# Layer 0 of a convolution-attention hybrid: the sums over whole cells as 64x64 matrices for two heads, and four buffers for the reciprocals

## The chip, the cores and the metric

The kernel runs on one core of one Trainium2 chip. The metric is the device time of the whole program in microseconds (us), from one launch, as the median of several runs. The engines are named as in the profile: PE is TensorE (matmuls), PEld its weight loads, DVE is VectorE, ACT is ScalarE, POOL is GpSimd, SP is SyncE, which here only issues DMAs. L816 means line 816 of the kernel before.

## The reference

The program has two layers on an image of 256 channels and 64 x 64 pixels, all in f32. The change is in layer 0 alone. There, after a group norm, q, k and v are made by 256 x 256 projections, q and k go through a sigmoid, and v is divided by its norm. There are 8 heads of 32 channels. For each pixel and each of three window sizes (64, 32 and 16 pixels wide) the products k vᵀ of all pixels in a box around the pixel are summed, and the pixel's q is multiplied with that sum and divided by q times the sum of k:

```
q = sigmoid(q); k = sigmoid(k); v = v / max(norm(v), 1e-12)
Ik = integral(k); Ikv = integral(einsum('bfhw,bghw->bfghw', k, v))
for w in (1, 2, 4):
    wk, wkv = box(Ik, 64 // w), box(Ikv, 64 // w)
    attn = einsum('bdhw,bdfhw->bfhw', q, wkv)
    outs.append(attn / (einsum('bdhw,bdhw->bhw', q, wk)[:, None] + 1e-6))
o = concatenate(outs); x = x + Wout @ o + bout
```

Layer 1 (softmax attention over 4096 tokens, then an expert layer with two experts per token) follows and is not touched.

## The kernel before, in words

**Cells.** The image is cut into cells of 8 x 8 pixels. A token's place is a strip `ix` of 8 columns (NCH = 8 strips of 512 tokens), a band `b` of 16 rows (NB = 4 bands of 128 tokens), and a half `u` of that band (one cell of 64 tokens). A box of 64, 32 or 16 pixels reaches `r` = 4, 2 or 1 cells to each side (`REACH`). For a query in a given cell, a box holds some cells entirely, for all queries of the cell alike; at its rims it cuts through others. Cells held entirely enter through their sum of k vᵀ: a 32 x 32 matrix for each head, prepared in `ssum[r]` for r = 4 and 2. Cells that are cut enter through scores: kᵀq for the cell, times a 0/1 mask, times v.

**Stages.** Heads are worked on in two halves of four (`g` = 0, 1), so that four heads fill 128 partitions. For each half, `prepare` makes q, k, v, the cell sums and the denominators (`rec`); `attend` then works through the windows in the order r = 2, r = 4, r = 1. For r = 2 and r = 4 it has two stages: first passes by rows of cells (bands 1, 2, 0, 3), then strips of columns, `ix` from 0 to 7. The change is in the passes by rows of cells.

**One pass.** Two PSUM banks, `accs[0]` and `accs[1]`, accumulate the two halves of a band, four heads on 128 partitions, 8 strips along the free dimension. The pass begins with the sums: for each u and ix, q of that cell times the sum of its whole cells. For r = 2 (L816) this is one 128 x 128 matrix for all four heads, with zeros off the diagonal, taken from the tile `blocks`. For r = 4 (L829) it is four 32 x 32 matrices straight from `ssum`. Then come steps of scores (L797, into four of six PSUM banks), masks (`masked`, L651 and L659), and the products with v (L841). The mask of heads 0 and 2 is applied by VectorE from PSUM; that of head 1, and of head 3 in every other step, by GpSimd from a copy that ScalarE makes. At the end ScalarE and VectorE copy the two banks into `raw` (L855).

**Order.** It is written out by hand. The matmuls of `use` (the sums, with the first step, and L841) are issued two steps after the scores that they go with (`behind`, `tick`). Besides, there is a list of `chores`, of which one is done after each step (`step_done`), and all that are left at the end of a pass (`finish`). `next_blocks` makes the chores that fill `blocks` for the next pass, one ScalarE activation for each head (L716): it copies the sums of all 8 strips and both halves, scaled by a 0/1 column that keeps one head's partitions. They are put at the front of the list as soon as the sums of the current pass are issued. `blocks` has one buffer, so the first of them waits until PE has read it. Other chores are the four parts of the reciprocal of `rec` (VectorE, L749), `turn_over` (which sends `rec` to DRAM and begins to fetch it back), and for each finished strip its division (L759, GpSimd) and its projection (L767).

**Reciprocals.** A division multiplies by `by`, a row of reciprocals spread over 32 partitions per head. SP fetches each by DMA (L738). There are two buffers; the next row is fetched when one has been used.

Of the kernel before, what the change touches and what calls it, by code (L numbers as in the profile page):

```python
# [22 lines left out]
F32 = mybir.dt.float32  # L23
# [7 lines left out]
P = 128  # L31
# [4 lines left out]
CH = 512  # L36
NCH = N // CH
# [4 lines left out]
CELL = SW * SW  # L42
D = 32
# [18 lines left out]
_MCELLS = [2 * r + 2 for r in REACH]  # L62
_MCELL0 = [sum(_MCELLS[:i]) for i in range(NW)]
_PARTS = {
    "": {"ident": P, "head": 4},
    "c": {"group": P, "xmask": 3 * SW, "ymask": SW * sum(_MCELLS), "ycut": 2 * SW},
    "k": {"sums": NCH // 4 * NW * D, "before8": CH, "sides": NB * (SW + IMG + 1)},
    "m": {"rank": NE, "iota": P, "before": P, "ones": P, "number": 1, "high": 2 * NT, "base": EARLY, "spare_early": 2 * EARLY, "spare": NU, "steps": N // SLOT, "unit": 3 * (NU - USUAL), "zero": 2 * NE},
# [1 line left out]
_AT, _W = {}, 0  # L70
# [6 lines left out]
def constants():  # L77

    out = np.zeros((P, _W), np.float32)
    p = np.arange(P)
    out[:, _AT["ident"]] = np.eye(P)
    out[:, _AT["group"]] = (p[:, None] // GRP == p[None, :] // GRP) / GRP
    out[:, _AT["head"]] = p[:, None] // D == np.arange(4)[None, :]
    a, b, c = p[:, None] % SW, p[:, None] // SW, np.arange(SW)[None, :]
    out[:, _AT["xmask"]] = np.concatenate([a >= 0 * c, a >= c, a < c], 1)
    rel = [np.arange(-SW * r, SW * r + BH)[None, :] for r in REACH]
    ys = [(b >= y - SW * r) & (b < y + SW * r) for r, y in zip(REACH, rel)]
    out[:, _AT["ymask"]] = np.concatenate(ys, 1)  # L90
    out[:, _AT["ycut"]] = np.concatenate([b % SW < c, b % SW >= c], 1)

    ns = range(NCH // 4 * NW)
    col = np.arange(D)[None, :]
    out[:, _AT["sums"]] = np.concatenate([col == 4 * n + p[:, None] // D for n in ns], 1)


    y, c = np.divmod(np.arange(CH)[None, :], SW)
    out[:, _AT["before8"]] = (b < y) & (a < c)
    c, y = np.arange(SW)[None, :], np.arange(IMG + 1)[None, :]  # L100
    out[:, _AT["sides"]] = np.concatenate(
        [np.concatenate([(a < c) & (b >= 0), BH * m + b < y], 1) for m in range(NB)], 1
    )
    out[:, _AT["rank"]] = NE - np.arange(NE)
    out[:, _AT["iota"]] = np.arange(P)
    out[:, _AT["before"]] = p[:, None] < p[None, :]
    out[:, _AT["ones"]] = 1
    out[:, _AT["number"]] = 1 + p[:, None]
    out[:, _AT["high"]] = np.arange(2 * NT)[None, :]
    out[:, _AT["base"]] = 1 + SLOT * np.arange(EARLY)  # L110
    spare = 1 + 2 * N + p[:, None] + P * np.arange(NU + 2 * EARLY)[None, :]
    out[:, _AT["spare"]], out[:, _AT["spare_early"]] = spare[:, :NU], spare[:, NU:]
    steps = SLOT * np.arange(N // SLOT)
    out[:, _AT["steps"]] = steps + np.minimum(steps, THIRD)
    unit = np.arange(USUAL, NU)
    out[:, _AT["unit"]] = np.concatenate([unit, (unit - THIRDS) // 2, unit - (unit - THIRDS) // 2])
    return out
# [3 lines left out]
def tile_conv_attn_hybrid(ctx: ExitStack, tc: tile.TileContext, a: dict, out: bass.AP):  # L121
    nc = tc.nc
# [15 lines left out]
    cst = constants_of("", const)  # L138
    ident = cst["ident"]
# [128 lines left out]
    with ExitStack() as phase:  # L268
# [28 lines left out]
        with (  # L297
# [3 lines left out]
            bank, _ = banks(ps)  # L301
# [323 lines left out]
        chores = []  # L625
# [70 lines left out]
        def attend(g, work, ps, qk, v, ssum, rec, woT):  # L696
# [3 lines left out]
            hs = [slice(D * h, D * (h + 1)) for h in range(4)]  # L700
            qcells = qT.rearrange("p (i n) -> p i n", n=CH)
# [1 line left out]

            blocks = work.tile([P, NCH, 2, 4, D], F32, name="blocks")
            passes = [(r, b) for r in (2,) for b in (1, 2, 0, 3)]

            def next_blocks():
                if not passes:  # L710
                    return []
                r, b = passes.pop(0)

                def block(h):
                    with tc.issue_after(latest_copy[0]) if latest_copy[0] else nullcontext():
                        nc.scalar.activation(  # L716
                            blocks[:, :, :, h, :],
                            ssum[r][:, :, 2 * b : 2 * b + 2, :],
                            AF.Copy,
                            scale=cst["head"][:, h : h + 1],  # L720
                        )

                return [lambda h=h: block(h) for h in range(4)]

            for f in next_blocks():
                f()
# [6 lines left out]
            def fetch():  # L733
                if order:
                    w, ix = order.pop(0)
                    by = work.tile([P, CH], F32, name="by", bufs=2)
                    row = D * (ix % 4) + 4 * (NCH // 4 * w + ix // 4)
                    nc.sync.dma_start(by, recs[row : row + 4, :].unsqueeze(1).to_broadcast([4, D, CH]))  # L738
                    held.append(by)

            def turn_over():
                nc.sync.dma_start(recs, rec)
                for _ in range(2):
                    fetch()

            def reciprocal(z):
# [7 lines left out]
            for w in windows:  # L754
                r = REACH[w]
# [22 lines left out]
                for b in (1, 2, 0, 3) if r > 1 else ():  # L778
                    accs = [bank() for _ in range(2)]
# [10 lines left out]
                    for step in steps:  # L790
                        scs = [score() for _ in range(4)]
                        at, places = 0, []
                        for n, i, lo, hi, kind in step:
                            for h in range(4):
                                for u in range(2):
                                    q0 = P * b + CELL * u
# [4 lines left out]
                                        start=True,  # L801
                                        stop=True,
                                        skip_group_check=True,
# [6 lines left out]
                        def use(places=places, sms=sms, accs=accs, begun=begun, b=b, last=step is steps[-1], raw=raw, r=r):  # L810
                            if not begun[0]:
                                begun[0] = True
                                if r == 2:
                                    for u, ix in ((u, ix) for u in range(2) for ix in range(NCH)):
                                        q0 = P * b + CELL * u
                                        nc.tensor.matmul(  # L816
                                            accs[u][:, CELL * ix : CELL * (ix + 1)],
                                            blocks[:, ix, u].rearrange("p h d -> p (h d)"),
                                            qcells[:, ix, q0 : q0 + CELL],
                                            start=ix == 0,  # L820
                                            stop=False,
                                            skip_group_check=True,
                                        )
                                    chores[:0] = next_blocks()
                                else:
                                    for u, ix in ((u, ix) for u in range(2) for ix in range(NCH)):
                                        for h in range(4):
                                            q0 = P * b + CELL * u
                                            nc.tensor.matmul(  # L829
                                                accs[u][hs[h], CELL * ix : CELL * (ix + 1)],  # L830
                                                ssum[r][hs[h], ix, 2 * b + u, :],
                                                qcells[hs[h], ix, q0 : q0 + CELL],
                                                start=ix == 0,
                                                stop=False,
                                                skip_group_check=True,
                                            )
                            for at, n, i, lo, hi, *_ in places:
                                for h in range(4):
                                    for u in range(2):
                                        us = slice(CELL * u, CELL * (u + 1))  # L840
                                        nc.tensor.matmul(  # L841
                                            accs[u][hs[h], CELL * lo : CELL * hi],
                                            v[us, i, hs[h]],
                                            sms[h][us, at : at + n],
                                            start=False,
                                            stop=last and at == places[-1][0],
                                            skip_group_check=True,
                                        )
                            if last:

                                finish()
                                for u in range(2):
                                    q0 = P * b + CELL * u

                                    (nc.vector.tensor_copy if u else nc.scalar.copy)(  # L855
                                        raw[:, :, q0 : q0 + CELL], accs[u].rearrange("p (i n) -> p i n", n=CELL)
                                    )
# [4 lines left out]
                for ix in range(NCH):  # L862
# [16 lines left out]
                    for step in steps:  # L879
                        scs = [score() for _ in range(4)]  # L880
                        at, places = 0, []
                        for n, i, c0, c1, *mk in step:

                            rows = CELL if len(step) == 1 else P
                            for h in range(4):
                                for u in range(0, P, rows):
# [4 lines left out]
                                        start=True,  # L891
                                        stop=True,
# [1262 lines left out]
```

## Time and profile before

| | |
|---|---|
| median of 3 runs | 2709.99 us (2706.1 to 2723.75) |
| profiled execution | 2709.02 us |
| its span, first to last instruction | 2707.1 us |
| PE busy | 2624.4 us (97%) |
| DVE busy | 1880.5 us (69%) |
| ACT busy | 1518.1 us (56%) |
| POOL busy | 817.9 us (30%) |
| mean granted TensorE clock | 0.990 |
| layer 0 in the span | up to about 964 us (last projection L767 at 964.4) |
| `attend`, first half: passes of r = 2, of r = 4 | about 128 to 189 us, about 260 to 324 us |
| `attend`, second half: the same | about 598 to 657 us, about 728 to 791 us |

How to read the profile's rows. A group of instructions has its line, engine, operation and tiles (output <- inputs), shapes (partitions x elements), a count, and the idle time of its engine before it, with what ended that idle time behind the arrow. For PE, 32\*64 means 32 rows and 64 columns of the array in use. An f32 matmul leaves two records, each a weight load and a matmul, so counts are twice those of the code. The busy time of overlapping matmuls is more than what passes by the clock; the time from one group's start to the next one's is the surer measure. In a table of stretches, each column is an engine's busy time with its number of instructions, and the granted clock is 1.00 at full speed.

### The profile page before, as it was taken

To read this page: it belongs to the slowest core of one execution; us is meant where nothing else is said; L and a number is where in the kernel's file an instruction comes from. 1 tells how busy PE (TensorE), PEld (TensorE's weight loads), DVE (VectorE), ACT (ScalarE), POOL (GpSimd) and SP (SyncE) were. 2 spreads that over 40 slices of the span, in tenths; PEclk is the share of its full clock that TensorE was granted. 3 is DMA by queue.
4 is the path that set the end of the run, shared out by engine and by line. 5 is a ranking of instruction groups with operands and counts; after the bars stand their busy time and mean duration, and the time that the engine had idled before them with its cause. 6 is when DMAs were issued, how large, how long until landed. Compare 5 with 4: busy or idle time off the path is not lost.

```text
span 2707.1 us, 70743 instructions
## 1 busy us (share of the span) xinstructions
PE 2624.4 (97%) x30398; PEld 1221.8 (45%) x30398; DVE 1880.5 (69%) x2570; ACT 1518.1 (56%) x2079; POOL 817.9 (30%) x919
## 2 busy tenths in 40 slices
PE   6999999999999999999999999999999999999995
PEld 5465436746544654111212121212121278888884
DVE  6868788586878866888888889888888871111114
ACT  3342323234232435999898989898989842222222
POOL 2067777306777731010000100000001122222220
PEclk9899999999999999999999999999999999999996
DMA  5000000000000000555555555555556645555555
GB/s 148 7 19 26 10 29 22 12 13 23 26 9 31 22 22 13 113 115 118 110 114 114 118 109 118 105 118 118 126 114 151 153 142 197 173 200 170 191 175 196
DMA packets 114461, 256.56 MB, mean 95 GB/s; under 512 B 19890, under 2 KB 76440, under 8 KB 100052
## 3 DMA queue, kind: packets, MB, share of 16 engines
q0 software_dynamic: 22240, 132.66, 23.4%
q1 hardware_dynamic: 84724, 110.30, 12.5%
q10 hardware_dynamic: 7168, 8.92, 1.0%
q8 instruction: 242, 3.96, 0.6%
q14 instruction: 87, 0.71, 0.1%
HBM read 118.64 MB, written 17.86 MB: 50 GB/s over the span
## 4 chain that ended last, share of the span: by engine, by line
PE 91%; DVE 4%; DMA 3%; issue 1%; ACT 1%; POOL 0%; ACTq 0%; SPq 0%; DVEq 0%; POOLq 0%
PE ps_three L1860 19%; PE ps_acc L1819 19%; PE ps_sc L887 8%; PE ps_yp L1528 8%; PE ps_hp L1511 7%; PE ps_acc L903 7%; PE ps_sc L767 3%; PE ps_sc L797 3%; PE ps_acc L841 3%; PE ps_two L441 2%; PE ps_mm L1303 2%; DMA yrows<-v,qk 2%; PE ps_two L534 1%; PE ps_acc L816 1%; PE ps_three L1794 1%; PE ps_mm L1318 1%
## 5 line engine op out<-in xcount | busy, mean ns | idle before, releaser
L1860 PE MATMUL ps_three<-qk 32*64 32x512 f32 x6144 | 563.2, 612 | 2.3 <-DVE t L1798 1.3
L1860 PE MATMUL ps_one<-qk 32*64 32x512 f32 x2048 | 556.3, 613 | 0.2 <-ACT pe L1869 0.2
L1892 DVE TENSOR_TENSOR act<-act,pe 128x2048 f32<-128x2048 f32 x195 | 447.3, 2294 | 82.5 <-ACT pe L1872 51.6
L1872 ACT ACTIVATE pe<-ps_three 128x1536 f32<-128x1536 f32 x330 | 477.3, 1446 | 0.0
L651 ACT COPY sm<-ps_sc 128x384 f32<-128x384 f32 (+2 forms) x418 | 212.9, 539 | 452.4 <-PE ps_sc L887 323.0
L659 DVE TENSOR_TENSOR sm<-ps_sc,mask 128x512 f32<-128x512 f32 (+3 forms) x788 | 343.3, 499 | 64.7 <-PE ps_sc L887 62.3
L659 POOL TENSOR_TENSOR sm<-sm,mask 128x192 f32<-128x192 f32 (+4 forms) x444 | 349.9, 819 | 113.3 <-ACT sm L651 113.2
L1892 DVE TENSOR_TENSOR act<-act 128x2048 f32<-128x2048 f32 x150 | 343.8, 2292 | 51.4 <-ACT act L1872 37.9
L1880 POOL DMA_DIRECT2D pe<-pe x108 | 93.4, 865 | 939.8 <-ACT pe L1872 610.4
L1819 PE MATMUL ps_acc<-pe,v 128*32 128x512 f32 x2640 | 351.6, 604 | 0.0
L1514 ACT ACTIVATE v<-ps_hp,qk 128x256 f32<-128x256 f32 (+1 forms) x256 | 123.1, 481 | 342.6 <-PE ps_hp L1511 342.6
L1860 PEld LDWEIGHTS ps_three<-qk 32*64 32x64 f32 x6144 | 112.6, 129 | 414.5 <-ACT pe L1869 244.0
L1872 ACT ACTIVATE act<-ps_three 128x1536 f32<-128x1536 f32 x182 | 263.1, 1446 | 0.0
L1528 PE MATMUL ps_yp<-qk,v 128*128 128x256 f32 (+1 forms) x1088 | 241.7, 380 | 0.0
L1511 PE MATMUL ps_hp<-qk 128*128 128x256 f32 (+1 forms) x1024 | 236.8, 389 | 2.8 <-ACT v L1514 1.7
L887 PE MATMUL ps_sc<-qk 32*128 32x256 f32 (+5 forms) x3456 | 233.2, 445 | 0.1
L1869 ACT ACTIVATE pe<-ps_one 128x512 f32<-128x512 f32 x330 | 197.5, 598 | 58.3 <-PE ps_one L1860 33.8
L1528 PEld LDWEIGHTS ps_yp<-qk,v 128*128 128x128 f32 (+1 forms) x1088 | 200.3, 187 | 30.7 <-issue 1.3
L903 PE MATMUL ps_acc<-sm,v 128*32 128x256 f32 (+4 forms) x2816 | 211.7, 407 | 0.1
L659 POOL TENSOR_TENSOR sm<-sm,ycut 128x512 f32<-128x512 f32 (+3 forms) x130 | 144.4, 1133 | 214.0 <-ACT sm L651 213.7
L1511 PEld LDWEIGHTS ps_hp<-qk 128*128 128x128 f32 x1024 | 180.7, 189 | 52.7 <-ACT v L1514 12.8
L1819 PE MATMUL ps_acc<-act,v 128*32 128x512 f32 x1456 | 193.9, 604 | 0.0
(364 smaller groups left out, 2908.8 us busy)
## 6 DMA issues: line engine op xcount, KB each, us to landing
pe<-pe POOLq DMA_DIRECT2D x108, 1024.0 KB, 7.6
qk<-in_L_ffn_W SPq DMA_DIRECT2D x64, 1024.0 KB
by<-recs SPq DMA_DIRECT2D x48, 256.0 KB
rows<-in_x SPq DMA_DIRECT2D x16, 256.0 KB
qk<-in_L_ffn_b SPq DMA_DIRECT2D x32, 128.0 KB
y<-yrows SPq DMA_DIRECT2D x8, 512.0 KB
y<-yrows ACTq DMA_DIRECT2D x8, 512.0 KB
rec<-recs SPq DMA_DIRECT2D x60, 64.0 KB
```

What stands on the lines that cost most here:

```text
L651: copied = nc.scalar.copy(sm[:, :used], sc[:, :used])
L659: done = engine.tensor_mul(to, of, mk.unsqueeze(1).to_broadcast(list(to.shape)))
L887: nc.tensor.matmul(scs[h][u : u + rows, at : at + n], kT[hs[h], P * i + u : P * i + u + rows], qT[hs[h], CH * ix + CELL * c0 : CH * ix + C ...
L903: nc.tensor.matmul(acc[hs[h], CELL * c0 : CELL * c1], v[:, i, hs[h]], sms[h][:, at : at + n], start=not begun[0], stop=last and at == plac ...
L1511: nc.tensor.matmul(hp[:, :n], w1[:, k, tok(m)], x_now[:, k, :n], start=k == 0, stop=k == KC - 1)
L1514: done["gelu"] = nc.scalar.activation(hid[:, m, :n], hp[:, :n], AF.Gelu, bias=cols[:, m : m + 1]).ins
L1528: product = nc.tensor.matmul(yp[:n], hid[:, m, P * j : P * j + n], w2[:, m, :], start=m == 0, stop=m == NH - 1)
L1819: nc.tensor.matmul(to[D * hd : D * (hd + 1), :], lhsT(hd), rhs(hd), start=start, stop=stop, skip_group_check=True,)
L1860: nc.tensor.matmul(to[CELL * u : CELL * (u + 1), :], qk[hs, 1, g, P * i + CELL * u : P * i + CELL * (u + 1)], qk[hs, 0, g, chunk(qc)], sta ...
L1869: first = nc.scalar.activation(head(pe, 0), one, AF.Exp, scale=C**-0.5)
L1872: nc.scalar.activation(pe[:, CH:], three.rearrange("p h n -> p (h n)"), AF.Exp, scale=C**-0.5).ins
L1892: latest[:] = [nc.vector.tensor_add(total, total, weights_of[r, i]).ins]
```

## The change

For both r = 2 and r = 4, the sums of a pass are now 64 x 64 matrices for two heads: two heads' 32 x 32 sums on the diagonal, zeros in the two other corners. Each pair (u, ix) has two of them, one for partitions 0 to 63 and one for partitions 64 to 127, each on its own rows and columns of the array. So a pass has 32 matmuls for its sums; it had 16 for r = 2 and 64 for r = 4.

`blocks` is half as large and is filled by two activations in place of four, one for the even and one for the odd heads, scaled by a new constant of two columns (`odd`). The list of passes it is filled for now includes r = 4: eight passes for each half of the heads. The fill for the first pass of r = 4 is added in the last pass of r = 2. The rows of reciprocals have four buffers instead of two, and four are fetched at first.

```diff
-    "": {"ident": P, "head": 4},
+    "": {"ident": P, "head": 4, "odd": 2},
...
+    out[:, _AT["odd"]] = p[:, None] // D % 2 == np.arange(2)[None, :]
...
-            blocks = work.tile([P, NCH, 2, 4, D], F32, name="blocks")
-            passes = [(r, b) for r in (2,) for b in (1, 2, 0, 3)]
+            blocks = work.tile([P, NCH, 2, 2, D], F32, name="blocks")
+            passes = [(r, b) for r in (2, 4) for b in (1, 2, 0, 3)]
...
-                            scale=cst["head"][:, h : h + 1],
+                            scale=cst["odd"][:, h : h + 1],
...
-                return [lambda h=h: block(h) for h in range(4)]
+                return [lambda h=h: block(h) for h in range(2)]
...
-                    by = work.tile([P, CH], F32, name="by", bufs=2)
+                    by = work.tile([P, CH], F32, name="by", bufs=4)
...
-                for _ in range(2):
+                for _ in range(4):
                     fetch()
...
-                                if r == 2:
-                                    for u, ix in ((u, ix) for u in range(2) for ix in range(NCH)):
-                                        q0 = P * b + CELL * u
+                                for u, ix in ((u, ix) for u in range(2) for ix in range(NCH)):
+                                    q0 = P * b + CELL * u
+                                    for two in (slice(0, 2 * D), slice(2 * D, 4 * D)):
                                         nc.tensor.matmul(
-                                            accs[u][:, CELL * ix : CELL * (ix + 1)],
-                                            blocks[:, ix, u].rearrange("p h d -> p (h d)"),
-                                            qcells[:, ix, q0 : q0 + CELL],
+                                            accs[u][two, CELL * ix : CELL * (ix + 1)],
+                                            blocks[two, ix, u].rearrange("p h d -> p (h d)"),
+                                            qcells[two, ix, q0 : q0 + CELL],
                                             start=ix == 0,
                                             stop=False,
                                             skip_group_check=True,
                                         )
-                                    chores[:0] = next_blocks()
-                                else:
-                                    for u, ix in ((u, ix) for u in range(2) for ix in range(NCH)):
-                                        for h in range(4):
-                                            q0 = P * b + CELL * u
-                                            nc.tensor.matmul(
-                                                accs[u][hs[h], CELL * ix : CELL * (ix + 1)],
-                                                ssum[r][hs[h], ix, 2 * b + u, :],
-                                                qcells[hs[h], ix, q0 : q0 + CELL],
...
+                                chores[:0] = next_blocks()
```

More of the change, by code (lines that the diff above doesn't have):

```diff
@@ L823, in use @@
                                         )
-                                    chores[:0] = next_blocks()
-                                else:
-                                    for u, ix in ((u, ix) for u in range(2) for ix in range(NCH)):
-                                        for h in range(4):
-                                            q0 = P * b + CELL * u
-                                            nc.tensor.matmul(
-                                                accs[u][hs[h], CELL * ix : CELL * (ix + 1)],
-                                                ssum[r][hs[h], ix, 2 * b + u, :],
-                                                qcells[hs[h], ix, q0 : q0 + CELL],
[L833 to L836, printed above, removed]
+                                chores[:0] = next_blocks()
                             for at, n, i, lo, hi, *_ in places:
```

## The prediction

> **What bounds the kernel now.** I read the chain that ended last first, since only time on it counts.
>
> ```profile
> PE 91%; DVE 4%; DMA 3%; issue 1%; ACT 1%; POOL 0%; ACTq 0%; SPq 0%; DVEq 0%; POOLq 0%
> PE ps_three L1860 19%; PE ps_acc L1819 19%; PE ps_sc L887 8%; PE ps_yp L1528 8%; PE ps_hp L1511 7%; PE ps_acc L903 7%; PE ps_sc L767 3%; PE ps_sc L797 3%; PE ps_acc L841 3%; PE ps_two L441 2%; PE ps_mm L1303 2%; DMA yrows<-v,qk 2%; PE ps_two L534 1%; PE ps_acc L816 1%; PE ps_three L1794 1%; PE ps_mm L1318 1%
> ```
>
> TensorE carries 91% of the chain. The line that the change removes, L816 (the sums of the passes with r = 2), is itself on it with 1%, about 27 us. Its counterpart for r = 4, L829, is not named. So the time rides on what these sums cost on PE. Next I cut the first half (g = 0) into stretches, each from one pass's sums to the next: four passes of r = 2, then two of r = 4.
>
> ```profile
> core 0: us, PE busy (x) PEld busy (x) DVE busy (x) ACT busy (x) POOL busy (x), PEclk, DMA share, GB/s
> 134.40:152.10 17.70, 16.81 (x549) 12.97 (x544) 11.22 (x21) 7.84 (x14) 11.21 (x12) 1.00 0.02 4
> 152.10:168.60 16.50, 16.18 (x537) 12.43 (x529) 9.41 (x19) 7.84 (x14) 10.40 (x12) 1.00 0.15 52
> 168.60:179.50 10.90, 9.59 (x297) 8.06 (x289) 6.56 (x13) 5.63 (x11) 5.84 (x6) 1.00 0.02 5
> 179.50:188.70 9.20, 9.20 (x208) 6.92 (x208) 3.19 (x9) 2.43 (x5) 3.86 (x6) 1.00 0.01 2
> 266.70:283.20 16.50, 15.93 (x432) 7.82 (x424) 11.40 (x20) 4.82 (x9) 10.60 (x10) 1.00 0.06 20
> 283.20:296.80 13.60, 13.60 (x424) 6.40 (x416) 9.21 (x17) 5.30 (x10) 10.62 (x10) 1.00 0.01 4
> ```
>
> PE is busy for nearly the whole of each stretch, at full granted clock (1.00); no other engine exceeds four fifths. Third, the timeline of PE around the sums of one pass of each kind: how long until the next kind of matmul starts, and what released it.
>
> ```profile
> 152.11 3.79 PE L816 MATMUL ps_acc<-qk,blocks 128*128 128x64 f32 x32
> 155.82 1.10 PE L841 MATMUL ps_acc<-sm,v 64*32 64x192 f32 x48
> ...
> 283.21 2.12 PE L829 MATMUL ps_acc<-qk,ssum 32*32 32x64 f32 x128
> 285.26 0.98 PE L841 MATMUL ps_acc<-sm,v 64*32 64x448 f32 x16
> ...
> 296.81 1.99 PE L829 MATMUL ps_acc<-qk,ssum 32*32 32x64 f32 x128
> 298.73 0.98 PE L841 MATMUL ps_acc<-sm,v 64*32 64x448 f32 x16
> ```
>
> From the first sum to the next L841, r = 2 takes 155.82 - 152.11 = 3.71 us (seven of its eight passes, the eighth 4.00 with a pause inside). r = 4 takes 298.73 - 296.81 = 1.92 us (six of eight; 2.05 and 2.67 where a pause fell in). In all, 30.0 and 16.2 us. Each f32 matmul has two records, so 16 matmuls make 32 and 64 make 128. The large form is the slow one. The reason shows in the instructions of single lines (durations are min/median/max):
>
> ```profile
> L816 PEld LDWEIGHTS ps_acc<-qk,blocks x256: 186/192/192, 134.4 to 650.5; 128*128 128x128 f32 x128
> L816 PE MATMUL ps_acc<-qk,blocks x256: 217/275/323, 134.4 to 650.6; 128*128 128x64 f32 x128
> ...
> L829 PEld LDWEIGHTS ps_acc<-qk,ssum x1024: 101/105/105, 266.7 to 779.7; 32*32 32x32 f32 x171
> L829 PE MATMUL ps_acc<-qk,ssum x1024: 211/214/238, 266.7 to 779.8; 32*32 32x64 f32 x171
> ...
> L797 PEld LDWEIGHTS ps_sc<-qk x2688: 127/131/227, 128.2 to 785.2; 32*64 32x64 f32 x192
> ```
>
> A load lasts 105, 131 and 192 ns for 32, 64 and 128 columns: some 77 ns of latency and 0.81 to 0.95 ns a column, so about 27, 54 and 110 ns of streaming. Matmuls of L829 and L816 stream 64 elements. Records of L829 start in fours, 56 ns from four to four, so 64 elements take about 56 ns. Pairs of L816 start 3.71/32 = 116 ns apart, which is its load: it is bound by weights, with the matmul hidden beside them.
>
> **The change part by part.** *The sums.* After it a pass of either kind has 16 places (8 column strips, 2 halves u), each with two 64x64 matmuls on separate rows and columns of the array: 32 matmuls, 64 pairs of records. Neither row shows a 64x64 form, so it is bounded from both sides. If both tiles run together and each load runs beside the matmul ahead of it, a round of two records costs the longer of 54 (load) and 56 (stream), and a pass has 32 rounds, as L829 has now (4 tiles a round). That gives L829's 1.92 us plus a longer first load (27 ns): 1.95 us. From above: nothing overlaps, 64 x (54 + 56) = 7.0 us.
>
> Two rules of the Trainium skill speak against the low end. *TensorE: Matmul & The Clock Gate* (Part 3, "What overlaps and what doesn't") says that a weight load overlaps with running matmuls only where the row group differs. Then the second record of a tile has its load in the open: 32 x 110 = 3.5 us a pass, nearly what r = 2 costs today, and +1.6 us for each pass of r = 4. The rows say otherwise: L829's rounds are 56 ns where load plus stream on one tile would be 83, and L816's are 116 where they would be 166. *TensorEngine Tiling (Array Packing)* (Restrictions and Gotchas, "PSUM Pressure") says that different row tiles cannot access one PSUM bank at once. The two tiles here write two halves of one bank. Run singly, 64 x 56 = 3.6 us. But L829's four row tiles write four quarters of one bank now, and 128 records of 211 ns fit into 1.99 us. I take 1.95 us, by L829, the nearest row: same stream, same bank, same number of rounds.
>
> r = 2: 30.0 - 8 x 1.95 = -14.4 us. r = 4: 8 x 0.03 = +0.2 us against its common 1.92; where the pauses fall I leave alone.
>
> Is the r = 2 part really time won? L816 gives the other engines time to catch up, so I look at who would be late. In the pass at 168.58 the masks on VectorE end at 170.3, ScalarE's copies at 169.6, GpSimd's at 171.3. With 1.95 us the sums end at 170.5. The first L841 behind them needs only masks made one or two steps earlier (GpSimd's at 169.0); those ending at 171.3 are due with the third L841. The same holds at 134 and 152 us. I count it in full.
>
> *The copies that fill blocks.* Before: 4 per pass x 4 passes x 2 halves = 32 of 0.72 us on ScalarE; after: 2 x 8 x 2 = 32. No work is added, half moves. In r = 2 it relieves one wait:
>
> ```profile
> 177.62 1.34 ACT L716 ACTIVATE blocks<-ssum,cst 128x512 f32<-128x512 f32 x2
> ...
> 178.85 0.58 ACT L855 COPY raw<-ps_acc 128x512 f32<-128x512 f32 x1
> ...
> 179.49 3.79 PE L816 MATMUL ps_acc<-qk,blocks 128*128 128x64 f32 x32 [1.31 <-ACT raw L855]
> ```
>
> The pass of band 0 has three steps, too few for four copies. The last two are flushed ahead of the copy that frees the accumulator, and PE stands 1.31 us (1.23 in the other half). Two copies fit into the steps; the accumulator's copy can then start about 1.1 us earlier, when VectorE's does (177.75). I take -1.1 x 2 = -2.2 us; bounds -2.5 and 0.
>
> The first fill of each half is two copies instead of four, but the first scores are ready only at 130.3, when all four are done today (130.1): zero. In r = 4, two copies per pass are new. The first waits until the sums have read the old blocks, with ScalarE's next score copies queued behind it and GpSimd's masks behind those. At 296.8 the copies in front end at 298.1, the sums at 298.8, so the copy runs to 299.5; the next score copy starts at 300.7. The second, behind that copy, would run from about 301.2 to 301.9; the next is due at 302.6. ScalarE works 5.3 of 13.6 us there. Nothing; if the cover failed, 0.7 us x 16 = 11 us at most. The first r = 4 pass gets its blocks in r = 2's last pass, some 80 us early. The chores inserted there push VectorE's reciprocals forward by two steps and one projection back by two, within passes that flush them anyway: zero.
>
> *Four reciprocal buffers.* Who the multiplications by them waited for:
>
> ```profile
>   DVE raw L913: 7.8, 18
>   PE ps_acc L903: 2.7, 2
> ```
>
> Never for a DMA: a row is fetched when the one two ahead is used, 7 us or more early. SP has two more 0.5 us issues up front, on a queue with nothing urgent, and as many fewer later. Zero either way, as for the two constant columns.
>
> Sum: -14.4 + 0.2 - 2.2 = -16.4 us. The profiled execution took 2709.0 us (span 2707.1, 1.9 outside), 1 us under the median. So 2692.6, and 2694 for a median, 0.6% less: inside the 1% that a measurement of this kernel can tell from no change.
>
> **The rivals.**
> 1. *The gain is real and goes through* (70%): 2694, own range 2689 to 2700.
> 2. *The gain is partly covered by the next wait* (15%): masks are late once the sums are shorter. For: VectorE waits for scores only 73 us over all L797 groups, and L797 waits 17 us for VectorE to free banks. Against: PE is busy for 88 to 100% of these stretches, and the 88 is the wait for ScalarE described with the copies. Half the 14.4 us is lost and none of the 2.2 comes: 2703; all lost: 2710.
> 3. *A load does not hide beside the matmul on its own tile* (11%), the slower side. Place: all 16 blocks of sums. Price: 32 x 110 = 3.5 us plus 0.15 for the change of form, 3.65 each, 58 us against 46: +12, so 2722. It decides from a round of (46.2/16 - 0.15)/32 = 86 ns on: below that the change gains, above it loses. If also both tiles ran singly, 16 x 7.1 = 114 us, +67: 2777 (3%).
> 4. *It does not do what it says* (1%): only if the trace showed a form other than 64x64.
>
> **How the numbers follow.** Likeliest: 2694. Rival 2 sets the upper end at 2711; the runs before spread from 2706 to 2724, which adds some us below case 1: 2687. That leaves out rival 3 and half the tails. Over 1% faster (below 2683) needs 27 us, nearly all that the r = 2 sums take today: 2%. Over 1% slower (above 2737) needs the full serial case or a new stall in each of the 16 passes: 7%. Within: 91%.
>
> **What would show it.** Right: 64*64 rows on one line, 64 records per pass, 1.9 to 2.0 us until L841 follows, in r = 2 and r = 4 alike; the 1.3 us wait for ScalarE at band 3 gone; layer 0 ending some 16 us earlier. Wrong: rounds near 110 ns, or L797 waiting longer for VectorE behind the sums, or ScalarE's score copies in r = 4 standing behind blocks.

## The result

The changed kernel takes 2700.1 us in the median (2696.7 to 2702.2, 17 runs), the kernel before 2713.5 us in the same series (2706.1 to 2725.7). The ratio is 0.9946, 95% interval 0.9937 to 0.9956: 0.54% faster, 14.7 us of 2714 (12 to 17); the medians themselves are 13.4 us apart. The interval leaves no change out, though the gain is less than the 1% that the prediction took as the least it could tell. It is close to the 16.4 us forecast. The sum behind it was less right than its total.

The profiled executions took 2709.02 and 2699.12 us. The one of before was among its shorter ones, so the two profiles differ by 9.9 us, and what follows explains 10 us, not the 14.7. The chain of work that ended last, after:

```profile
PE 91%; DVE 4%; DMA 3%; issue 1%; ACT 1%; POOL 0%; ACTq 0%; SPq 0%; DVEq 0%; POOLq 0%
PE ps_three L1849 19%; PE ps_acc L1808 19%; PE ps_sc L876 8%; PE ps_yp L1517 8%; PE ps_hp L1500 7%; PE ps_acc L892 7%; PE ps_sc L768 3%; PE ps_sc L798 3%; PE ps_acc L830 3%; PE ps_two L442 2%; PE ps_mm L1292 2%; DMA yrows<-v,qk 2%; PE ps_two L535 1%; PE ps_acc L817 1%; PE ps_three L1783 1%; PE ps_mm L1307 1%
```

It is the same chain. L817 is now the line of the sums, L798 of the scores (before L797), L830 of the products with v (before L841). The instructions of L817:

```profile
L817 PEld LDWEIGHTS ps_acc<-qk,blocks x1024: 129/135/136, 134.7 to 769.2; 64*64 64x64 f32 x171
L817 PE MATMUL ps_acc<-qk,blocks x1024: 212/218/268, 134.7 to 769.3; 64*64 64x64 f32 x171
```

The form is 64*64, the load 135 ns, as for the 64 columns of L797 before. From the first sum to the next L830 a pass takes 2.01 us in 13 of 16 passes (2.20 to 2.30 in three with r = 2):

```profile
149.32 2.37 PE L817 MATMUL ps_acc<-qk,blocks 64*64 64x64 f32 x64
151.61 1.10 PE L830 MATMUL ps_acc<-sm,v 64*32 64x192 f32 x48
152.64 1.08 PE L798 MATMUL ps_sc<-qk 32*64 32x192 f32 x35
154.73 0.47 PE L798 MATMUL ps_sc<-qk 32*64 32x128 f32 x13 [1.01 <-issue]
155.13 1.10 PE L830 MATMUL ps_acc<-sm,v 64*32 64x192 f32 x48
156.16 0.91 PE L798 MATMUL ps_sc<-qk 32*64 32x192 f32 x32
157.00 1.05 PE L830 MATMUL ps_acc<-sm,v 64*32 64x192 f32 x35
159.01 0.44 PE L830 MATMUL ps_acc<-sm,v 64*32 64x128 f32 x13 [0.96 <-issue]
...
260.99 2.08 PE L817 MATMUL ps_acc<-qk,blocks 64*64 64x64 f32 x64
263.00 0.98 PE L830 MATMUL ps_acc<-sm,v 64*32 64x448 f32 x16
```

Two things stand out. PE stops twice inside a group, for 1.01 and 0.96 us, and the releaser reads "issue": the instruction waited for nothing that the profile shows. Such pauses stood in r = 2 before, too, but were shorter in this half (0.58 us at most). The second is what is not there: in r = 4 the pause behind the sums of band 1 is gone. Before it read:

```profile
266.68 1.99 PE L829 MATMUL ps_acc<-qk,ssum 32*32 32x64 f32 x128
268.60 0.98 PE L841 MATMUL ps_acc<-sm,v 64*32 64x448 f32 x15
270.15 0.56 PE L841 MATMUL ps_acc<-sm,v 64*32 64x448 f32 x1 [0.57 <-issue]
```

The whole stages tell the same, once before and once after. The columns are those of the table in the prediction (stretch, length, then PE, PEld, DVE, ACT, POOL, clock, DMA); the rows are r = 2 in both halves, then r = 4 in both halves:

```profile
128.30:188.00 59.70, 56.38 (x1700) 44.31 (x1700) 33.57 (x62) 26.61 (x48) 33.90 (x34) 0.97 0.05 17
598.00:655.50 57.50, 54.23 (x1696) 43.19 (x1696) 33.55 (x62) 26.52 (x48) 33.81 (x34) 1.00 0.05 18
260.30:322.50 62.20, 61.62 (x1732) 29.07 (x1728) 43.19 (x76) 21.04 (x40) 45.60 (x41) 1.00 0.04 12
727.80:790.20 62.40, 61.86 (x1732) 29.09 (x1728) 43.38 (x76) 21.03 (x40) 45.65 (x41) 1.00 0.04 12
```

```profile
128.40:182.30 53.90, 50.74 (x1825) 38.12 (x1825) 33.74 (x62) 23.18 (x43) 33.78 (x34) 0.96 0.08 29
591.40:646.10 54.70, 49.98 (x1826) 36.97 (x1826) 33.78 (x62) 23.10 (x42) 33.99 (x34) 1.00 0.08 28
254.60:315.90 61.30, 61.30 (x1476) 29.31 (x1472) 43.27 (x76) 25.04 (x46) 45.59 (x41) 1.00 0.04 12
718.40:779.70 61.30, 61.30 (x1476) 29.31 (x1472) 43.26 (x76) 25.05 (x46) 45.60 (x41) 1.00 0.04 12
```

r = 2 goes from 117.2 to 108.6 us, r = 4 from 124.6 to 122.6: 10.6 us together. The strips between and the rest of the program are as long as before. But r = 2 should have lost more. Its sums fell from 30.0 to 16.8 us, and PE's wait for ScalarE ahead of band 3 is gone as well (before, then after):

```profile
179.49 3.65 PEld L816 LDWEIGHTS ps_acc<-qk,blocks 128*128 128x128 f32 x32 [1.66 <-ACT raw L855]
...
174.65 0.60 ACT L844 COPY raw<-ps_acc 128x512 f32<-128x512 f32 x1
...
175.31 2.15 PEld L817 LDWEIGHTS ps_acc<-qk,blocks 64*64 64x64 f32 x64 [0.39 <-ACT raw L844]
```

The weight load waits 0.39 us (1.66 before), and the idle time that PE's matmuls had there, 1.31 us and 1.23 us in the two halves, is gone: 2.5 us. So 13.2 + 2.5 = 15.7 us were taken from PE in r = 2, and only 8.6 came out. About 7 us went somewhere, not evenly: some 1.8 us in the first half and 5.3 us in the second.

### The profile page after: what moved, and what is told of

The parts are those of the page before. It is cut to its first block, busy times and chain, and to the rows that moved or that the text cites. A ratio compares the mean times of both kernels' runs of the same rounds, so it can differ in the third digit from the quotient of the medians.

```text
span 2697.3 us, 70229 instructions
## 1 busy us (share of the span) xinstructions
PE 2616.6 (97%) x30142; PEld 1210.2 (45%) x30142; DVE 1880.0 (70%) x2570; ACT 1518.4 (56%) x2079; POOL 815.8 (30%) x919
## 4 chain that ended last, share of the span: by engine, by line
PE 91%; DVE 4%; DMA 3%; issue 1%; ACT 1%; POOL 0%; ACTq 0%; SPq 0%; DVEq 0%; POOLq 0%
PE ps_three L1849 19%; PE ps_acc L1808 19%; PE ps_sc L876 8%; PE ps_yp L1517 8%; PE ps_hp L1500 7%; PE ps_acc L892 7%; PE ps_sc L768 3%; PE ps_sc L798 3%; PE ps_acc L830 3%; PE ps_two L442 2%; PE ps_mm L1292 2%; DMA yrows<-v,qk 2%; PE ps_two L535 1%; PE ps_acc L817 1%; PE ps_three L1783 1%; PE ps_mm L1307 1%
## 5 line engine op out<-in xcount | busy, mean ns | idle before, releaser
L1881 DVE TENSOR_TENSOR act<-act 128x2048 f32<-128x2048 f32 x150 | 343.8, 2292 | 51.5 <-ACT act L1861 36.9
```

The source lines that it names most:

```text
L1881: latest[:] = [nc.vector.tensor_add(total, total, weights_of[r, i]).ins]
```

## The experiments

**The theory formed from the two traces.** PE's program comes by DMA while PE runs, in packets of 16384 bytes on a queue that the profile calls "instruction". In r = 2, 14 packets go with about 1825 pairs of load and matmul, 130 a packet; before, 13 went with 1700. (The Trainium skill, *Runtime: NRT & Kernel Launch*, section "Instruction fetch mechanics", gives 256 instructions a block, which is 128 pairs.) The starts of these packets, taken from the trace's DMA records, first half of r = 2:

```
before   gaps, us: 6.85 4.29 3.38 3.72 5.06 3.51 3.75 3.72 3.47 4.82 3.77 6.89
after    gaps, us: 4.28 3.50 3.45 3.47 4.39 4.40 3.47 3.43 3.51 3.41 3.46 3.75 3.35
```

In this half, nine of the 13 gaps after the change are 3.35 to 3.51 us, whatever PE has to do. In the second half they are looser, 3.37 to 4.63 us with a median of 3.79, so 3.45 us is about the shortest spacing and not the mean, which is 3.7 to 3.9 us. The packet itself takes only 0.9 to 1.4 us. 3.45 us for 128 pairs is 27 ns a pair; the groups of r = 2 take 48 pairs in 1.03 us, 21 ns a pair, when the instructions are there, and PE can take them faster still: the 128 pairs of L829 went in 1.92 us, 15 ns a pair. My reading: packets come no faster than that, and this now bounds r = 2. A pass's sums became 1.7 us shorter but have 32 pairs more, which would cost 32 x 27 ns = 0.9 us.

**The rival** is the prediction's second case: masks come late once the sums no longer cover them. A third question is the four buffers, whose rows go out at 147 us, where the gaps read 4.39 and 4.40.

**One kind of pass alone.** r = 2 with 64x64 and r = 4 as before; then the reverse. Both with two buffers.

```diff
-            passes = [(r, b) for r in (2, 4) for b in (1, 2, 0, 3)]
+            passes = [(r, b) for r in (2,) for b in (1, 2, 0, 3)]
...
+                                if r == 2:
                                     for u, ix in ((u, ix) for u in range(2) for ix in range(NCH)):
...
+                                else:
+                                        for h in range(4):
...
+                                                ssum[r][hs[h], ix, 2 * b + u, :],
```

> 64x64 sums in the passes with r = 2 alone; r = 4 keeps its four 32x32 matrices, and the reciprocals two buffers. Theory (instruction loading): in the passes with r = 2, PE's instructions arrive in blocks of 16 KB (128 pairs of load and matmul) no faster than about one in 3.45 us, so shorter sums with twice the instructions give only part of the 13.2 us that they save on PE. Some 9 us in the profile, and pauses of PE inside its groups as in the changed kernel; ratio to the kernel before about 0.996. Rival (masks come late): also some 9 us, but L841 waiting for GpSimd or L797 waiting for VectorE by 4 us more than before. If nothing is lost: 16 us, ratio 0.994.

Measured: 2702.3 us (5 runs), ratio 0.9955 (0.9941 to 0.9969). From the first start to the last end, r = 2 took 52.9 and 53.2 us, r = 4 62.3 and 62.9.

```diff
-            blocks = work.tile([P, NCH, 2, 2, D], F32, name="blocks")
+            blocks = work.tile([P, NCH, 2, 4, D], F32, name="blocks")
...
+                                if r == 2:
...
+                                        accs[u][:, CELL * ix : CELL * (ix + 1)],
+                                        blocks[:, ix, u].rearrange("p h d -> p (h d)"),
...
+                                else:
...
+                                            blocks[two, ix, u, :2].rearrange("p h d -> p (h d)"),
```

> 64x64 sums in the passes with r = 4 alone; r = 2 keeps one 128x128 matrix, two buffers. Theory (instruction loading): the sums themselves get 0.1 us longer per pass, but 64 fewer pairs per pass take away the pauses of about 1 us that stood behind the sums of 128 pairs; 1 to 2 us less than before, ratio 0.9993 to 0.9996. Rival (the sums' own length alone decides): 0 to 1 us longer.

Measured: 2712.6 us (21 runs), ratio 0.9991 (0.9983 to 0.9999). Measured in the same way, r = 4 took 61.42 us in each half, to the hundredth what it takes in the changed kernel. The sums there are 2.01 us a pass, 0.09 more than the common 1.92 of four 32x32, and yet the stage is 1 us shorter: what went are the pauses in and behind the bursts of 128 pairs. So r = 2 brings some 12 us and r = 4 some 2, which add up to about the change (16.0 us by its ratio for both with two buffers, below; the intervals reach 2 to 4 us to each side). These runs do not yet tell the theory from the rival. The waits speak for the theory. In the second half's r = 2, before and after:

```profile
PEld ps_acc L841 <- issue: 4.7, 15, 1.2
PEld ps_sc L797 <- DVE sm L659: 2.7, 6, 0.9
PEld ps_sc L797 <- issue: 1.9, 9, 0.3
```

```profile
PEld ps_acc L830 <- issue: 6.5, 18, 1.0
...
PEld ps_sc L798 <- issue: 4.5, 11, 1.3
...
PEld ps_sc L798 <- DVE sm L660: 3.3, 7, 1.1
...
PE ps_acc L830 <- issue: 1.7, 3, 0.8
PE ps_sc L798 <- issue: 1.7, 4, 1.0
```

The columns are the total, the number and the longest, in us. Waits for VectorE grew by 0.6 us, GpSimd's masks are not named, and what grew are waits for nothing shown: 6.6 to 11.0 us on weight loads.

**As short on PE, but with more instructions.** Both kinds of pass use four 32x32 matrices straight from the sums, 128 pairs a pass; nothing fills `blocks`, and the reciprocals have two buffers.

```diff
-            passes = [(r, b) for r in (2, 4) for b in (1, 2, 0, 3)]
+            passes = []
...
-                                    for two in (slice(0, 2 * D), slice(2 * D, 4 * D)):
+                                    for h in range(4):
...
-                                            blocks[two, ix, u].rearrange("p h d -> p (h d)"),
-                                            qcells[two, ix, q0 : q0 + CELL],
+                                            ssum[r][hs[h], ix, 2 * b + u, :],
+                                            qcells[hs[h], ix, q0 : q0 + CELL],
```

> Both kinds of pass with four 32x32 matrices straight from the sums (64 matmuls a pass, no blocks to fill), two buffers. The sums take 1.92 us of PE, as short as 64x64, with twice their instructions. Theory (instruction loading): 64 pairs more in each pass with r = 2 than in the changed kernel, two blocks of 3.45 us in each half, partly in slack: 4 to 7 us longer per half, 8 to 13 us and about 2 more for r = 4, so a ratio to the kernel before of 0.998 to 1.000. Rival (the sums' length on PE or the masks decide): as fast as the changed kernel or 1 us faster, ratio 0.994 to 0.995.

Measured: 2715.1 us (21 runs), ratio 1.0004 (0.9996 to 1.0012): the whole gain is gone. The rival had 0.994 to 0.995. The stages of r = 2 in this kernel:

```profile
128.20:188.30 60.10, 50.45 (x2080) 37.12 (x2080) 33.63 (x62) 17.20 (x33) 33.84 (x34) 1.00 0.05 17
599.50:660.20 60.70, 51.04 (x2080) 37.16 (x2080) 34.02 (x62) 17.21 (x33) 34.18 (x35) 1.00 0.05 18
```

PE is busy for only 50.5 of 60.1 us, and no other engine for more than 34. ScalarE has 6 us less to do than in the changed kernel, and the masks are the same. PE waits here for its instructions: 16 packets, with a median of 3.63 us from one to the next, which is 58 of the 60 us. The trace ties the pauses to the packets. After the first packet of this stage has landed in the first half, PE has eleven pauses (neither load nor matmul) of more than 0.25 us, and each of them ends 1.25 to 1.54 us after a packet has landed. The two of 1.01 and 0.96 us in the changed kernel end 1.42 and 1.45 us after one.

**The same streaming with fewer instructions.** In r = 2 eight matmuls of 64 elements become one of 512. The matrix of strip 0 stands in for all strips, so the sums of the other strips are left out there.

```diff
-                                    for two in (slice(0, 2 * D), slice(2 * D, 4 * D)):
...
+                                                accs[u][two, :],
+                                                blocks[two, 0, u].rearrange("p h d -> p (h d)"),
+                                                qcells[two, :, q0 : q0 + CELL],
```

> The changed kernel, but in the passes with r = 2 the 16 matmuls of 64 elements for each pair of heads become 2 of 512: the matrix of strip 0 is used for all eight strips, so the sums of the other strips in r = 2 are left out. PE streams as many elements (2 x 2 x 427 = 1.71 us against 1.79), with 8 pairs of records instead of 64. Theory (instruction loading): 56 pairs fewer in each of 8 passes are 3.5 blocks of 3.45 us, 12 us at most and 6 to 10 us with what other waits take back: faster than the changed kernel by 6 to 10 us, ratio to the kernel before 0.991 to 0.9925, and pauses inside PE's groups mostly gone. Rival (the sums' length on PE decides): 8 x 0.15 = 1.2 us faster than the changed kernel, ratio 0.994.

Measured: 2692.5 us (5 runs), ratio 0.9923 (0.9909 to 0.9936), 7.6 us under the changed kernel by the medians and 6.2 by the ratios, as the theory had it and not the 1.2 of the rival. r = 2 took 52.2 and 50.0 us. PE's sums still took 1.88 us a pass against 2.10, so 1.7 us of it come from the sums' length. More of the gaps between packets are above 4 us again (seven of 12 in the first half, three of 13 in the changed kernel). But the pauses did not mostly go, as was expected: in the second half weight loads still waited 10.7 us for "issue" (11.0 in the changed kernel), and in the first half three pauses of PE, 0.68 to 0.86 us long, stand between 145 and 162 us, while four rows of reciprocals are in flight. The stage got shorter with its number of pairs; it did not come free of waiting for them.

**Two buffers.** The changed kernel with `bufs=2` and two rows at first.

```diff
-                    by = work.tile([P, CH], F32, name="by", bufs=4)
+                    by = work.tile([P, CH], F32, name="by", bufs=2)
...
-                for _ in range(4):
+                for _ in range(2):
```

> The changed kernel with two buffers for the reciprocals instead of four, two rows fetched at first. Theory: the four rows of 256 KB go out while PE is short of instructions, and the blocks come 4.4 us apart instead of 3.45 as long as they are moved; with two rows one such gap of 0.95 us goes away in each half: 1 to 2 us faster than the changed kernel, ratio to the kernel before 0.994. Rival (buffers do nothing): equal to the changed kernel within 0.5 us, ratio 0.9946.

Measured: 2698.5 us (5 runs), ratio 0.9941 (0.9927 to 0.9955). The gaps read 4.85, 3.33 where four rows gave 4.39, 4.40. The difference from the changed kernel was too small for these runs, so both ran once more side by side:

> The changed kernel once more, beside the next two on one chip: 2700 us within 2, ratio to the kernel before 0.9946 within 0.001.

> The changed kernel with two buffers, once more. Theory (four rows at once cost some 2 us by slowing PE's instruction blocks): 1.5 to 2.5 us faster than the changed kernel. Rival (no difference): within 1 us of it.

Measured: 2700.0 and 2698.4 us (6 runs each), ratios 0.9945 and 0.994. By the means of all runs of these two kernels, on several chips, four rows cost 1.1 us more (interval -0.1 to 2.4). The direction agrees with the theory, the size is under what it gave, and the runs of these two kernels alone do not show it beyond their noise.

**The rows sent later.** First the calls alone were moved, behind the pass of band 0:

```diff
-            chores.append(turn_over)
...
                                 finish()
+                                if r == 2 and b == 0:
+                                    turn_over()
```

> The changed kernel, with the rows of reciprocals sent and fetched behind the third pass (band 0) of r = 2 instead of in the first and second; four buffers. Theory (instruction loading, slowed by the rows' DMAs): the two gaps of 4.4 us between instruction blocks in each half go back to 3.45; the last pass, which is short, takes up the DMAs: 1 to 4 us faster than the changed kernel, ratio to the kernel before 0.993 to 0.9942. Rival (the DMAs do not matter): as the changed kernel, 0.9946 within 0.0005. If the rows came too late for the first division, GpSimd would wait for them and the strips of r = 2 would grow beyond 72.3 us.

> The same late fetch with two buffers and two rows at first. Theory: 0 to 1 us from late_rows, the last pass of r = 2 a little shorter. Rival (the DMAs do not matter): as two_rows, 0.9941.

Measured: 2699.7 us, ratio 0.9947 (0.9933 to 0.996), and 2697.2 us, ratio 0.9939 (0.9925 to 0.9952). The theory's 1 to 4 us did not come with four rows. The profile shows why this tested nothing: the rows were not late.

```profile
L739 SPq DMA_DIRECT2D by<-recs x48: 500/505/730, 145.9 to 903.8; - x48
```

The first is issued at 145.9 us, in the changed kernel at 147.1. SP runs its own program and is held by nothing but the last part of the reciprocal; where a DMA stands among the other engines' instructions does not matter to it. The two-row form is a second sample of two buffers, in effect. With these two added, four rows cost 1.5 us more than two (28 and 16 runs, interval 0.4 to 2.6). The profiles agree: both halves of r = 2 together took 107.6 to 109.8 us in three profiles with 64x64 sums and four rows, and 106.1 to 107.7 in four with two rows sent at the same place.

So the reciprocals themselves were moved, with two buffers: three parts to band 2, the last part and the sending to band 3.

```diff
-            for i in range(4):
-                chores.append(lambda i=i: reciprocal(rec[:, tok(i)]))
-            chores.append(turn_over)
...
                                 chores[:0] = next_blocks()
+                                if r == 2 and b == 2:
+                                    chores.extend(lambda i=i: reciprocal(rec[:, tok(i)]) for i in range(3))
+                                if r == 2 and b == 3:
+                                    chores.insert(0, lambda: (reciprocal(rec[:, tok(3)]), turn_over()))
```

> Two buffers, and the reciprocals themselves moved: three of their parts to the pass of band 2, the last to that of band 3, since SP sends the rows as soon as the last part is made, wherever its DMA stands in the program. So the rows are moved while the last pass of r = 2 gives way to the strips, where PE has 72 us for some 950 pairs. Theory (DMAs slow the instruction blocks): the gaps of 4.0 to 4.8 us in the first passes go back to some 3.5, 1 to 3 us faster than with two buffers alone, ratio to the kernel before 0.993 to 0.994. Rival (those gaps have another cause): as two buffers alone, or slower by 1 us where a reciprocal on VectorE now stands in a shorter pass.

Measured: 2696.2 us (6 runs), ratio 0.9931 (0.9917 to 0.9945). That is 2.0 us below two buffers (interval 0.7 to 3.2), and the fastest kernel here that computes all of it. The gaps between packets moved with the rows, first half and second half:

```
changed kernel  at 144 to 157 us: 3.47 4.39 4.40   at 605 to 618 us: 3.78 4.63 4.25
late_recip      at 144 to 157 us: 3.47 3.64 3.43   at 605 to 618 us: 3.45 3.54 3.47   at 636 to 645 us: 4.42 4.32
```

The DMAs of the two kernels in the same stretch, 143 to 157 us, the changed kernel first (the first row is the busy share of the DMA engines in 40 slices):

```profile
DMA  0000100089000100222223222242222222222224
...
q1 hardware_dynamic: 555, 1.08, 20.4%
q8 instruction: 4, 0.07, 1.8%
```

```profile
DMA  0000100000000020000000000100000000100000
...
q8 instruction: 4, 0.07, 1.8%
```

With the 1.08 MB of `rec` and its rows gone from this stretch, the four instruction packets come some 3.5 us apart. This speaks for the rows' traffic, but it is weaker than the count of instructions: the stage became shorter in the second half alone (51.5 us against 54.7), while in the first, 53.6 against 53.9, later gaps of 3.7 to 4.2 us took back what the two early ones gave. The reciprocals themselves moved on VectorE as well, but PE gained nothing by that: in the first half its weight loads for the scores waited 3.1 us for VectorE, 2.8 in the changed kernel. How traffic holds packets up was not measured.

## Why the prediction was right, and where not

**The sums, r = 2 (-14.4 forecast).** -13.2 us: 1.95 us was taken, 2.01 measured (and three small pauses). Both of its disputed assumptions hold: a load of 64 columns runs beside the matmul ahead of it on the same tile, and the two tiles run together on one bank. 2.01 us for 32 rounds is at most 63 ns a round, where the rule on row groups that the prediction cites would give 110, and one tile at a time twice 56. Rival 3, the slower side, which decided from 86 ns on, is out.

**"I count it in full."** This is the step that failed: the r = 2 gain of 14.4 us was entered without a term for PE's instructions. I asked which engine would be late next and found none, and that was right: waits for masks hardly changed. I did not count instructions as something that PE waits for, though the trace of before showed it: pauses with the releaser "issue" in r = 2, the instruction queue on the page, and 128 records behind one another in r = 4. About 7 us of the 15.7 taken from PE in r = 2 were given back, comparing the two profiles. That is half of the 14.4, which is what rival 2 had priced, but it did not go to late masks. The runs put a size on it from both sides: 64 pairs more a pass, at the same length on PE, cost the whole gain; 56 fewer in r = 2 bring another 6 to 8 us, of which 1.7 are the sums' own length. Why packets come 3.4 to 3.9 us apart when each takes about 1 us stays open.

**The sums, r = 4 (+0.2 forecast).** -2 us. Again the number of instructions: 64 pairs fewer a pass outweigh sums that are 0.09 us longer. I had left the pauses alone; they went, and the stage came out at 61.42 us in every profile with 64x64 there, against 62.3 to 63.2 with 32x32.

**The wait at band 3 (-2.2 forecast).** -2.5, by the named mechanism. The copies that moved into r = 4 cost nothing, as said: that stage has PE busy for all its 61.3 us.

**Four buffers (zero either way).** Not quite: some 1.5 us lost (interval 0.4 to 2.6), it seems from the same resource that I had not put into the sum. That no one waits for `by` was true.

**The total.** In the profiles: -13.2 and -2.5 on PE in r = 2, some 7 given back, -2.0 in r = 4, -10.6 us together. By the ratio of all runs the change is 14.7 us. The difference is the kernel before, whose profiled execution was 4 to 5 us faster than its median. Its r = 2 is not always equally long: a profile of the kernel with r = 2 unchanged shows 119.8 us for both halves where that of before shows 117.4. What varies there from execution to execution was not tried. So the forecast of 16.4 us landed near the measured time with one term that was too good and two that were too careful, and it is luck that it came so near: set against the two profiles, it is 6 us too high.

## What to carry to other kernels

Where a stage issues small matmuls back to back, count its instructions beside its streaming time, and divide: here 128 pairs of load and matmul needed at least some 3.45 us to arrive, 27 ns a pair (3.7 to 3.9 us in the mean of a stage), and a stage that would run at 21 ns a pair is bound by that. A slow instruction can then be cheap cover for loading, and splitting it into quicker ones pays for only part of what it saves; having fewer, longer matmuls pays more than their streaming says. A pause whose releaser is "issue", in the middle of a group, is the sign; that such pauses end at a fixed time behind the landing of a packet on the instruction queue (here 1.2 to 1.5 us) is the evidence, and a run with more instructions and the same streaming is the test.

A DMA is not late because it stands later in the program: SP runs ahead to the last result that the transfer needs, so it is that result that has to be moved.

## What I had not expected of the hardware

- PE's instruction packets of 16 KB start 3.4 to 3.9 us apart while PE is short of them, although each takes only about 1 us. With the rows of reciprocals in flight single gaps were 4.2 to 4.9 us.
- In the kernel with only 32x32 matrices, PE was idle for 16% of r = 2 with every other engine below 60%.
- 64x64 tiles in f32, two on the diagonal of the array with 64 elements each, run at 63 ns a round, as four 32x32 do at 60: from 32 to 64 columns the width of the tile costs next to nothing. One of 128 columns took 116 ns.
